# The scan loop of a gated SSM with mixture of experts: a step of one state and two channel chunks in place of two states and one chunk

## The chip, the cores and the metric

The kernel runs on one core of a Trainium2 chip. The metric is the device time of one execution, in microseconds (us). Line numbers (L482) are those of the kernel before; PE is TensorE, DVE is VectorE, ACT is ScalarE, POOL is GpSimd, SP is the engine that issues most DMAs. A number such as 128x1024 is partitions by elements, all float32.

## What is computed

A batch is 512 positions of 512 channels, and there are four batches. Cut to what matters (ssm and ffn are the two layers):

```
x = x + tanh(g_xattn) * ssm(ctx, z=layernorm(x))
x = x + tanh(g_ffn)   * ffn(layernorm(x))

ssm:  u = silu(conv4(in_proj @ ctx))              # 512 channels x 512 positions
      dt, B, C = x_proj @ u;  delta = softplus(dt_proj @ dt + bias)
      for each of 16 states n, along the positions t:
          state_n = state_n * exp(delta_t * A_n) + (delta_t * u_t) * B_t[n]
          y_t    += state_n * C_t[n]
      y = (y + D * u) * silu(z)
ffn:  shared(x) + sum over the 3 best of 7 experts of weight_e * expert_e(x)
      expert(x) = (silu(x @ w1) * (x @ wg)) @ w2   # all 512 x 512
```

## The kernel before

**Layout.** Channels lie on partitions, in four chunks of 128 (NC = 4), and positions along the free dimension. The state recurrence is one scan instruction of DVE along 512 positions for each state and chunk: 16 x 4 = 64 scans a batch.

**The scan loop** (`loop(b, sums)`, L434 on) makes 32 steps a batch. A step is a pair of states (g0, g0 + 1) of one chunk c; the four chunks follow each other within a pair of states. In a step:

- `product` (L509, POOL, 128x1024): B of both states times delta*u of the chunk, into one of two buffers `h`. It is issued one step ahead, so it waits until the buffer's last reader, an add of the step before, is done.
- `decay` (L514, L520, ACT, two of 128x512): exp(delta*A) for each state, into one of two PSUM banks `da`; an exp waits until the scan that read its bank is done.
- two scans (L540, DVE, 128x512), state by state.
- `finish`, issued with the next step: the multiply by C (L467, DVE, 128x1024), and the sum over states. In loop 0 (batch 0) PE sums, with two identity matmuls (L480) into a PSUM bank for each chunk. In loops 1 to 3 DVE sums, with two adds (L482, 128x512) into the same 512 columns of y.

B and C are broadcast to all partitions by a load of 1 MB for a pair of states (`load_bc`, L256 on), two pairs ahead. `ready` (L493) prepares a chunk when its first step comes: `rest_of_z` (L299, L300) and `soft` (L308, L309) on DVE finish delta, `d_u` (L314, ACT) puts D*u into y, `mul` (L321, DVE) makes delta*u. `gate` (L456, DVE) multiplies y by silu(z) at the end of a chunk. Small closures such as silus wait in a list `later` until `flush` issues them. In loops 1 to 3 the pieces of the next layer's preparation (`ahead`: in_proj, conv, x_proj, soft and so on) are issued between the steps.

**The experts** (`moe`, `post`, `route`, `experts`). For each batch q after its loop: `post` turns y by PE (L606), adds it to x and takes statistics on DVE (L610 to L612), normalizes (L615), turns the result back (L623) and copies it by ACT (L626). `route` computes gate logits (pl L670, lg L672, pg L676), the three best on DVE (L689 to L727), counts by PE (pc L718, L719) and scatters rows to expert tiles by indirect DMAs of POOL (L782). `experts` does the shared expert (p1s and p2s L827, the silu sgs L925, hidden L928, pos L960), then 13 tiles of routed rows: turn (L816), copy (L821), p1 and p2 (p, L827), silu (h, L1054), gating (h, L999), turn and copy of h, po (L827), scaling (yo, L860, ACT) and an adding indirect DMA (L865, POOL). After the last full tile stands an If (L878) for the rest. Below, po_12 or h_12 is that of tile 12.

**The order** is written out by hand: each engine gets its instructions in the order in which the program issues them, and executes them in that order. `front` prepares batch 0, loop 0 runs alone, and then a small planner at the end of the kernel merges two generators, the slots of `moe` and the steps of `ssm`: each slot has a PE cost and a DVE cost, each step returns its DVE cost (3.6 in loop 0, 4.95 in the others, and what is issued with it), and steps are issued while their sum lags behind PE's (`while tV < tP`). So loops 1, 2 and 3 interleave with the experts of batches 0, 1 and 2, and the experts of batch 3 run alone.

```
    for slot in moe():
        ...
        tP += slot[0]
        tV += slot[1]
        must = len(slot) > 2 and slot[2]
        while tV < tP or must:
            must = False
            d = next(steps, None)
```

Of the kernel before, what the change touches and what calls it, by code (L numbers as in the profile page):

```python
# [16 lines left out]
P = 128  # L17
# [6 lines left out]
NG = 2  # L24
I32 = mybir.dt.int32
# [7 lines left out]
def gated_ssm_moe(  # L33
# [170 lines left out]
    class Layer:  # L204
# [51 lines left out]
        def load_bc(self, g0):  # L256
            bc = two.tile([P, 2, NG, L], F32, tag="bc", name=f"bc_{self.b}_{g0}")
            nc.sync.dma_start(bc, self.rows[:, g0 : g0 + NG, :].partition_broadcast(P))
            self.bcs[g0] = bc
# [107 lines left out]
    def front():  # L367


        l0, l1 = layers[0], layers[1]  # L370
        for c in range(NC):
            l0.in_proj(c)
        for c in range(2):
            l1.in_proj(c)
        for c in range(NC):
            l0.conv(c)
            if c > 0:
                l0.silu(c - 1)
        l0.silu(NC - 1)
        for c in range(2):  # L380
            l1.conv(c)
        l0.x_proj()
        l0.rows_out()
        l0.load_bc(0)
        l0.load_bc(NG)
        for c in range(NC):
            l0.dt_proj(c)
        l1.in_proj(2, ps_a.tile([P, L], F32, tag="da", name="pin_1_2"))
        l1.in_proj(3, ps_s.tile([P, L], F32, tag="s", name="pin_1_3"))
        for c in range(NC):  # L390
            l0.abs_relu(c, by_vector=True)
        for c in range(NC):
            l0.exp(c)
        for c in range(NC):
            l0.log(c, own=False)
        norm_x(0)
        for c in range(NC):
            l0.rest_of_z(c)
        l0.soft(0)
        l0.mul(0)  # L400
        l1.conv(2)
# [32 lines left out]
    def loop(b, sums):  # L434
# [16 lines left out]
        steps = [(g0, c) for g0 in range(0, NS, NG) for c in range(NC)]  # L451
# [6 lines left out]
        def finish(n, h):  # L458

            g0, c = steps[n]  # L460
            bc = ly.bcs[g0]
            cost = 0.0
            if sums is not None and n >= NC:
                next(todo, 0.0)
                next(early, None)
            hc = h if sums is None else held[-1][:, n % 2]
            nc.vector.tensor_tensor(hc, h, bc[:, 1], ALU.mult)  # L467
            if sums is None:
                if b - 1 in shared_done:

                    left = max(n_todo - done[0], 0)
                    for _ in range(max(1, -(-left // max(1, len(steps) - NC - n)))):
                        done[0] += 1
                        cost += next(todo, 0.0)
                if nxt is not None and g0 + NG == NS and 0 < c <= nxt.n_du:
                    nxt.mul(c - 1)
                    cost += 0.7
            for j in range(NG):
                if sums is not None:
                    nc.tensor.matmul(sums[c], ident, hc[:, j, :], start=False, stop=(g0 + j == NS - 1))  # L480
                else:
                    nc.vector.tensor_tensor(y[:, c, :], y[:, c, :], h[:, j, :], ALU.add)  # L482
            if sums is not None and g0 + NG == NS and c > 0:
                gate(c - 1)
            if c == NC - 1:
                ly.bcs.pop(g0)
                if g0 + 2 * NG < NS:
                    ly.load_bc(g0 + 2 * NG)
                elif nxt is not None:
                    nxt.load_bc(g0 + 2 * NG - NS)  # L490
            return cost

        def ready(layer, n):  # L493

            g0, c = steps[n]
            cost = 0.0
            if g0 == 0 and layer.n_soft == c:
                layer.soft(c)
                cost += 1.4
            if g0 == 0 and layer.n_mul == c:  # L500
                layer.mul(c)
                cost += 0.7
            return cost

        def product(layer, n):

            g0, c = steps[n]
            h = two.tile([P, NG, L], F32, tag="h", name=f"h_{layer.b}_{g0}_{c}")
            nc.gpsimd.tensor_tensor(  # L509
                h, layer.bcs[g0][:, 0], layer.u[:, c, :].unsqueeze(1).to_broadcast([P, NG, L]), ALU.mult  # L510
# [3 lines left out]
        def decay(layer, n):  # L514

            g0, c = steps[n]
            layer.das[n] = []
            for k in range(g0, g0 + NG):
# [6 lines left out]
        for n, (g0, c) in enumerate(steps):  # L525
            cost = 3.6 if sums is not None else 4.95
# [9 lines left out]
            if sums is not None and g0 == 0:  # L536
                nc.tensor.matmul(sums[c], ident, y[:, c, :], start=True, stop=False)
            h = ly.hs.pop(n)
            for j, da in enumerate(ly.das.pop(n)):
                nc.vector.tensor_tensor_scan(h[:, j, :], da, h[:, j, :], 0.0, ALU.mult, ALU.add)  # L540
# [4 lines left out]
            elif nxt is not None and nxt.n_mul > 0:  # L545
                product(nxt, 0)
                decay(nxt, 0)
            if b == 0 and g0 == 0:
                if c == 0:
                    nxt.conv(NC - 1)  # L550
                    for k in range(NC):
                        later.append(lambda k=k: nxt.silu(k))
                    szs = silus_x(b)
                if c == 1:
                    flush()
            if g0 + NG == NS:
                if nxt is not None and nxt.n_soft == NC:
                    nxt.d_u(c)
                if c > 0 and sums is None:
                    flush()  # L560
                    gate(c - 1)
                    cost += 0.7
# [3 lines left out]
            if b > 0 and g0 == 10:  # L566
                norm_x(b, c)
                cost += 0.9
            if b > 0 and g0 == 12 and c == 1:
# [6 lines left out]
        gate(NC - 1)  # L576
# [551 lines left out]
    held[-1] = wpool.tile([P, 2, NG, L], F32, tag="w0", name="hc")  # L1128
# [70 lines left out]
```

## Time and profile before

| what | value |
|---|---|
| median of 3 runs | 1161.34 us (1160.76 to 1167.23) |
| profiled execution, its own time | 1164.13 us |
| its span (first to last instruction) | 1161.9 us |
| mean granted TensorE clock | 0.938 of full |
| PE, DVE busy from 180 to 951 us (771 us) | 660 and 643 us |
| a step of loop 0, scan to scan | 3.58 us |
| a step of loops 1 to 3 with nothing between | 4.96 us |

The span is the time that the trace covers; 2.2 us lie around it. Loop 0 ends near 179 us; the last step of loop 3 lies before 951 us, where the routing of batch 3 begins. In a profile line of the timeline the columns are: start, busy time (us), engine, line, operation, output<-inputs, size, count, and in brackets the idle time of the engine before it and what ended it.

### The profile page before, as it was taken

The numbers are of one execution on the slowest core, as the hardware profiler recorded it, in microseconds if no ns is written. First come the engines' busy times: TensorE is split into PE (matmuls) and PEld (weight loads), VectorE is DVE, ScalarE is ACT, GpSimd is POOL, SyncE is SP. The second block draws the span as 40 slices with busy tenths as digits, with TensorE's granted clock in tenths as the row PEclk, the third lists the DMA queues.
The fourth block names the chain that finished last, engine by engine and source line by source line (L and its number), as shares of the span: only waits on it lengthen the run. The fifth ranks groups of instructions, "written<-read, shape, count | busy, mean of one in ns | idle before, by whom it ended". The sixth has DMA issues, their size and how long they took to land. (4 is left out here: it accounts for less than half of the span.)

```text
span 1161.9 us, 8955 instructions
## 1 busy us (share of the span) xinstructions
PE 960.8 (83%) x2504; PEld 427.8 (37%) x2504; DVE 816.7 (70%) x1093; ACT 537.9 (46%) x747; POOL 470.7 (41%) x311
## 2 busy tenths in 40 slices
PE   7376555678799897986999994987998979999993
PEld 3122112333344443433444441433443534444441
DVE  5889996977889998866989996969999502100000
ACT  4565343253676774434586762435657220122211
POOL 0255651272344655451444644554666214011111
PEclk9689898889899998988999997988999999999998
DMA  4159221098499988387799975498999757899974
GB/s 126 46 178 377 113 72 55 14 348 290 152 315 303 300 292 234 118 314 238 246 311 322 353 225 144 173 301 273 316 349 345 219 175 247 299 346 325 332 226 101
DMA packets 138427, 276.30 MB, mean 238 GB/s; under 512 B 17262, under 2 KB 17262, under 8 KB 138110
## 3 DMA queue, kind: packets, MB, share of 16 engines
q1 hardware_dynamic: 126846, 248.91, 61.4%
q0 software_dynamic: 11328, 26.42, 9.9%
q8 instruction: 26, 0.43, 0.1%
q10 hardware_dynamic: 192, 0.26, 0.1%
q14 instruction: 35, 0.29, 0.1%
HBM read 234.85 MB, written 44.91 MB: 241 GB/s over the span
## 5 line engine op out<-in xcount | busy, mean ns | idle before, releaser
L509 POOL TENSOR_TENSOR h<-bc,home 128x1024 f32<-128x1024 f32 x128 | 304.5, 2380 | 376.2 <-DVE home L482 268.7
L827 PE MATMUL p<-w,turned_x 128*128 128x512 f32 x832 | 381.7, 603 | 22.6 <-ACT h L1054 18.7
L540 DVE TENSOR_TENSOR_SCAN h<-da,h 128x512 f32<-128x512 f32 x256 | 298.3, 1207 | 18.6 <-POOL h L509 13.1
L520 ACT ACTIVATE da<-home,a_neg 128x512 f32<-128x512 f32 x256 | 174.5, 689 | 281.8 <-DVE h L540 279.4
L827 PEld LDWEIGHTS p<-w,turned_x 128*128 128x128 f32 x832 | 155.0, 193 | 206.1 <-issue 172.7
L827 PE MATMUL po<-w,turned_h 128*128 128x512 f32 x416 | 190.1, 600 | 19.3 <-ACT yo L860 16.4
L865 POOL DMA_INDIRECT acc<-yo,row x52 | 93.3, 1794 | 220.4 <-ACT yo L860 168.8
L482 DVE TENSOR_TENSOR home<-home,h 128x512 f32<-128x512 f32 x192 | 132.6, 691 | 5.9
L999 DVE TENSOR_TENSOR h<-h,p 128x512 f32<-128x512 f32 x52 | 35.1, 675 | 143.5 <-PE p L827 142.3
L467 DVE TENSOR_TENSOR h<-h,bc 128x1024 f32<-128x1024 f32 x96 | 130.6, 1360 | 1.1
L480 PE MATMUL sum<-hc,ident 128*128 128x512 f32 x128 | 69.5, 669 | 56.4 <-DVE hc L467 56.4
L827 PEld LDWEIGHTS po<-w,turned_h 128*128 128x128 f32 x416 | 75.7, 192 | 98.4 <-issue 75.9
L821 ACT COPY turned_x<-pt_x 128x512 f32<-128x512 f32 x52 | 30.2, 581 | 103.8 <-PE pt_x L816 103.7
L960 PE MATMUL pos<-w_s,home 128*128 128x512 f32 x128 | 66.2, 674 | 10.5 <-DVE home L928 7.8
L782 POOL DMA_INDIRECT xs<-xn,place x48 | 56.7, 1182 | 29.1 <-issue 15.9
L827 PE MATMUL p1s<-home,w_s 128*128 128x512 f32 x128 | 61.6, 626 | 5.5 <-ACT sgs L925 5.5
L520 ACT ACT_TABLE_LOAD x51 | 65.4, 1283 | 0.9
L860 ACT ACTIVATE yo<-po,weight 128x512 f32<-128x512 f32 x52 | 35.6, 684 | 62.2 <-PE po L827 48.6
L480 PEld LDWEIGHTS sum<-hc,ident 128*128 128x128 f32 x128 | 23.6, 205 | 101.5 <-DVE hc L467 79.4
L827 PE MATMUL p2s<-home,w_s 128*128 128x512 f32 x128 | 57.5, 592 | 0.0
L233 DVE SCALAR_TENSOR_TENSOR home<-pin,pr,home 128x511 f32<-128x511 f32 (+2 forms) x48 | 35.7, 748 | 23.8 <-ACT home L229 22.7
L821 ACT COPY turned_h<-pt_h 128x512 f32<-128x512 f32 x52 | 30.0, 578 | 46.9 <-PE pt_h L816 46.9
(137 smaller groups left out, 810.1 us busy)
## 6 DMA issues: line engine op xcount, KB each, us to landing
w<-in_w_dram SPq DMA_DIRECT2D x104, 1024.0 KB, 7.8
w<-in_wg_dram SPq DMA_DIRECT2D x52, 1024.0 KB, 8.7
bc<-rows SPq DMA_DIRECT2D x32, 1024.0 KB, 10.4
xt<-xs SPq DMA_DIRECT2D x52, 256.0 KB, 5.6
xs<-empty SPq DMA_DIRECT2D x6, 1560.0 KB
w_s<-in_ws_dram SPq DMA_DIRECT2D x8, 1024.0 KB, 9.4
xx<-in_x_dram SPq DMA_DIRECT2D x4, 1024.0 KB, 11.1
w_s<-in_wsg_dram SPq DMA_DIRECT2D x4, 1024.0 KB
```

What stands on the lines that cost most here:

```text
L233: nc.vector.scalar_tensor_tensor(xc[:, k:], pin[:, 0 : L - k], pr[:, c, last - k : last - k + 1], xc[:, k:], ALU.mult, ALU.add,)
L467: nc.vector.tensor_tensor(hc, h, bc[:, 1], ALU.mult)
L480: nc.tensor.matmul(sums[c], ident, hc[:, j, :], start=False, stop=(g0 + j == NS - 1))
L482: nc.vector.tensor_tensor(y[:, c, :], y[:, c, :], h[:, j, :], ALU.add)
L509: nc.gpsimd.tensor_tensor(h, layer.bcs[g0][:, 0], layer.u[:, c, :].unsqueeze(1).to_broadcast([P, NG, L]), ALU.mult)
L520: nc.scalar.activation(da, layer.delta[:, c, :], AF.Exp, scale=a_neg[:, c, k : k + 1])
L540: nc.vector.tensor_tensor_scan(h[:, j, :], da, h[:, j, :], 0.0, ALU.mult, ALU.add)
L782: put = nc.gpsimd.indirect_dma_start(xs[q % 2], bass.IndirectOffsetOnAxis(ap=place[:, t, k : k + 1], axis=0), xns[:, t, :], None)
L821: nc.scalar.copy(t, pt)
L827: nc.tensor.matmul(p[:, 0:n], lhs(c), rhs(c), start=(c == 0), stop=(c == NC - 1))
L865: nc.gpsimd.indirect_dma_start(acc, bass.IndirectOffsetOnAxis(ap=slot_of[q][1][:, i : i + 1], axis=0), yo, None, compute_op=ALU.add,)
L960: nc.tensor.matmul(pos[t], hTs[:, c, ts(t, P)], ws.t[2][:, c, :], start=(c == 0), stop=(c == NC - 1))
```

## The change

A step becomes one state k of two neighbouring chunks c0 and c0 + 1 (W = 2). There are 32 steps as before. For each load of B and C the order is (first state, chunks 0 and 1), (second state, chunks 0 and 1), (first, 2 and 3), (second, 2 and 3). The product and the multiply by C read one state's row for both chunks. The two scans of a step write two chunks, so in loops 1 to 3 one add of 128x1024 into two chunks of y takes the place of two adds of 128x512; in loop 0 the two matmuls of a step go to two banks. With this:

- `front` does soft and mul of chunks 0 and 1 before conv(2) (before: chunk 0 alone), and `ready` does two chunks at a time, also at the end of loop 0.
- the gates come later: in loop 0 those of chunks 0 and 1 with the last step but one, in loops 1 to 3 those of 0 and 1 with the last two steps, and those of 2 and 3 at the end.
- D*u and delta*u of the next layer are made in the last three steps, one a step and two in the last.
- the planner's cost of a step of loops 1 to 3 is 4.8 in place of 4.95.

The diff in full:

```diff
--- before.py
+++ after.py
@@ -22,6 +22,7 @@
 TOPK = 3
 EPS = 1e-5
 NG = 2
+W = 2
 I32 = mybir.dt.int32
 
 CW, CB, DTB, DD, AL = 0, 4, 5, 6, 7
@@ -256,7 +257,7 @@
         def load_bc(self, g0):
             bc = two.tile([P, 2, NG, L], F32, tag="bc", name=f"bc_{self.b}_{g0}")
             nc.sync.dma_start(bc, self.rows[:, g0 : g0 + NG, :].partition_broadcast(P))
-            self.bcs[g0] = bc
+            self.bcs[g0 // NG] = bc
 
 
 
@@ -396,8 +397,9 @@
         norm_x(0)
         for c in range(NC):
             l0.rest_of_z(c)
-        l0.soft(0)
-        l0.mul(0)
+        for c in range(W):
+            l0.soft(c)
+            l0.mul(c)
         l1.conv(2)
 
 
@@ -448,7 +450,11 @@
             todo = ahead(nxt)
         n_todo, done = 1 + NC + (NC + 2) + 2 * (NC // 2), [0]
         szs = None
-        steps = [(g0, c) for g0 in range(0, NS, NG) for c in range(NC)]
+
+        steps = [
+            (g0 + j, c0) for g0 in range(0, NS, NG) for c0 in range(0, NC, W) for j in range(NG)
+        ]
+        per_load = NG * NC // W
 
         def gate(c):
 
@@ -457,73 +463,79 @@
 
         def finish(n, h):
 
-            g0, c = steps[n]
-            bc = ly.bcs[g0]
+            k, c0 = steps[n]
+            i = n % per_load
             cost = 0.0
-            if sums is not None and n >= NC:
+            if sums is not None and n >= per_load:
                 next(todo, 0.0)
                 next(early, None)
             hc = h if sums is None else held[-1][:, n % 2]
-            nc.vector.tensor_tensor(hc, h, bc[:, 1], ALU.mult)
+            c_k = ly.bcs[k // NG][:, 1, k % NG, :]
+            nc.vector.tensor_tensor(hc, h, c_k.unsqueeze(1).to_broadcast([P, W, L]), ALU.mult)
             if sums is None:
                 if b - 1 in shared_done:
 
                     left = max(n_todo - done[0], 0)
-                    for _ in range(max(1, -(-left // max(1, len(steps) - NC - n)))):
+                    for _ in range(max(1, -(-left // max(1, len(steps) - per_load - n)))):
                         done[0] += 1
                         cost += next(todo, 0.0)
-                if nxt is not None and g0 + NG == NS and 0 < c <= nxt.n_du:
-                    nxt.mul(c - 1)
+                if nxt is not None and n >= last - W and nxt.n_mul < nxt.n_du:
+                    nxt.mul(nxt.n_mul)
                     cost += 0.7
-            for j in range(NG):
-                if sums is not None:
-                    nc.tensor.matmul(sums[c], ident, hc[:, j, :], start=False, stop=(g0 + j == NS - 1))
-                else:
-                    nc.vector.tensor_tensor(y[:, c, :], y[:, c, :], h[:, j, :], ALU.add)
-            if sums is not None and g0 + NG == NS and c > 0:
-                gate(c - 1)
-            if c == NC - 1:
-                ly.bcs.pop(g0)
-                if g0 + 2 * NG < NS:
-                    ly.load_bc(g0 + 2 * NG)
+            if sums is None:
+                nc.vector.tensor_tensor(y[:, c0 : c0 + W, :], y[:, c0 : c0 + W, :], h, ALU.add)
+            else:
+                for w in range(W):
+                    nc.tensor.matmul(sums[c0 + w], ident, hc[:, w, :], start=False, stop=(k == NS - 1))
+                if n == last - 1:
+                    for c in range(NC - W):
+                        gate(c)
+            if i == per_load - 1:
+                ly.bcs.pop(k // NG)
+                g = k // NG + 2
+                if g * NG < NS:
+                    ly.load_bc(g * NG)
                 elif nxt is not None:
-                    nxt.load_bc(g0 + 2 * NG - NS)
+                    nxt.load_bc(g * NG - NS)
             return cost
 
         def ready(layer, n):
 
-            g0, c = steps[n]
+            k, c0 = steps[n]
             cost = 0.0
-            if g0 == 0 and layer.n_soft == c:
-                layer.soft(c)
-                cost += 1.4
-            if g0 == 0 and layer.n_mul == c:
-                layer.mul(c)
-                cost += 0.7
+            for c in range(c0, c0 + W):
+                if k == 0 and layer.n_soft == c:
+                    layer.soft(c)
+                    cost += 1.4
+                if k == 0 and layer.n_mul == c:
+                    layer.mul(c)
+                    cost += 0.7
             return cost
 
         def product(layer, n):
 
-            g0, c = steps[n]
-            h = two.tile([P, NG, L], F32, tag="h", name=f"h_{layer.b}_{g0}_{c}")
+            k, c0 = steps[n]
+            h = two.tile([P, W, L], F32, tag="h", name=f"h_{layer.b}_{k}_{c0}")
+            b_k = layer.bcs[k // NG][:, 0, k % NG, :]
             nc.gpsimd.tensor_tensor(
-                h, layer.bcs[g0][:, 0], layer.u[:, c, :].unsqueeze(1).to_broadcast([P, NG, L]), ALU.mult
+                h, b_k.unsqueeze(1).to_broadcast([P, W, L]), layer.u[:, c0 : c0 + W, :], ALU.mult
             )
             layer.hs[n] = h
 
         def decay(layer, n):
 
-            g0, c = steps[n]
+            k, c0 = steps[n]
             layer.das[n] = []
-            for k in range(g0, g0 + NG):
+            for c in range(c0, c0 + W):
                 da = ps_a.tile([P, L], F32, tag="da", name=f"da_{layer.b}_{k}_{c}")
                 nc.scalar.activation(da, layer.delta[:, c, :], AF.Exp, scale=a_neg[:, c, k : k + 1])
                 layer.das[n].append(da)
 
         last = len(steps) - 1
         h_before = None
-        for n, (g0, c) in enumerate(steps):
-            cost = 3.6 if sums is not None else 4.95
+        for n, (k, c0) in enumerate(steps):
+            i = n % per_load
+            cost = 3.6 if sums is not None else 4.8
             if h_before is not None:
                 cost += finish(n - 1, h_before)
             if n not in ly.hs:
@@ -533,47 +545,50 @@
                 decay(ly, n)
             if n < last:
                 cost += ready(ly, n + 1)
-            if sums is not None and g0 == 0:
-                nc.tensor.matmul(sums[c], ident, y[:, c, :], start=True, stop=False)
+            if sums is not None and k == 0:
+                for c in range(c0, c0 + W):
+                    nc.tensor.matmul(sums[c], ident, y[:, c, :], start=True, stop=False)
             h = ly.hs.pop(n)
-            for j, da in enumerate(ly.das.pop(n)):
-                nc.vector.tensor_tensor_scan(h[:, j, :], da, h[:, j, :], 0.0, ALU.mult, ALU.add)
+            for w, da in enumerate(ly.das.pop(n)):
+                nc.vector.tensor_tensor_scan(h[:, w, :], da, h[:, w, :], 0.0, ALU.mult, ALU.add)
 
             if n < last:
                 product(ly, n + 1)
                 decay(ly, n + 1)
-            elif nxt is not None and nxt.n_mul > 0:
+            elif nxt is not None and nxt.n_mul >= W:
                 product(nxt, 0)
                 decay(nxt, 0)
-            if b == 0 and g0 == 0:
-                if c == 0:
-                    nxt.conv(NC - 1)
-                    for k in range(NC):
-                        later.append(lambda k=k: nxt.silu(k))
-                    szs = silus_x(b)
-                if c == 1:
-                    flush()
-            if g0 + NG == NS:
-                if nxt is not None and nxt.n_soft == NC:
+            if b == 0 and n == 0:
+                nxt.conv(NC - 1)
+                for c in range(NC):
+                    later.append(lambda c=c: nxt.silu(c))
+                szs = silus_x(b)
+            if b == 0 and n == 1:
+                flush()
+            if nxt is not None and nxt.n_soft == NC and n >= last - W and nxt.n_du < NC:
+
+                ready_du = (c0 + W) if n < last else NC
+                for c in range(nxt.n_du, min(nxt.n_du + (1 if n < last else W), ready_du)):
                     nxt.d_u(c)
-                if c > 0 and sums is None:
-                    flush()
-                    gate(c - 1)
-                    cost += 0.7
+            if n >= last - 1 and sums is None:
+                flush()
+                gate(n - last + 1)
+                cost += 0.7
             h_before = h
             if n == 2 and b > 0 and nxt is not None:
                 ctxs[b + 1] = load_ctx(b + 1)
-            if b > 0 and g0 == 10:
-                norm_x(b, c)
+            if b > 0 and k // NG == 5:
+                norm_x(b, i)
                 cost += 0.9
-            if b > 0 and g0 == 12 and c == 1:
+            if b > 0 and k // NG == 6 and i == 1:
                 szs = silus_x(b)
             yield cost
         if b == 0:
             for c in range(NC):
                 nxt.log(c, own=False)
         cost = finish(last, h_before)
-        gate(NC - 1)
+        for c in range(NC - W, NC):
+            gate(c)
         if b == 0:
             cost += ready(nxt, 0)
             product(nxt, 0)
@@ -1125,7 +1140,7 @@
 
 
 
-    held[-1] = wpool.tile([P, 2, NG, L], F32, tag="w0", name="hc")
+    held[-1] = wpool.tile([P, 2, W, L], F32, tag="w0", name="hc")
     front()
     held[0] = shared_weights(0)
     early = first_loads()
```

## The prediction

> **What bounds the kernel now.** I read busy times, then windows by stage, then the timeline inside one step and at each long wait of PE.
>
> ```profile
> PE 960.8 (83%) x2504; PEld 427.8 (37%) x2504; DVE 816.7 (70%) x1093; ACT 537.9 (46%) x747; POOL 470.7 (41%) x311
> L482 DVE TENSOR_TENSOR home<-home,h 128x512 f32<-128x512 f32 x192 | 132.6, 691 | 5.9
> ```
> ```profile
> 300.00:400.00 100.00, 95.29 (x258) 42.50 (x257) 91.89 (x111) 68.89 (x97) 48.21 (x24) 0.98 0.86 285
> 500.00:600.00 100.00, 86.71 (x208) 37.22 (x209) 76.42 (x90) 52.13 (x72) 38.68 (x23) 0.90 0.78 266
> 700.00:800.00 100.00, 75.14 (x184) 32.15 (x184) 76.50 (x120) 37.76 (x50) 48.84 (x40) 0.90 0.67 212
> 960.00:1060.00 100.00, 99.33 (x271) 46.51 (x270) 15.00 (x46) 14.59 (x26) 17.93 (x28) 1.00 0.89 304
> ```
>
> Window columns: length, busy PE, PEld, DVE, ACT, POOL, clock, DMA share, GB/s. Four stages follow. Until about 180 us loop 0 runs alone and DVE sets the pace. From 180 to 951 loops 1 to 3 are interleaved with the experts of batches 0 to 2. In mid-batch (300:400) PE is at 95 and DVE at 92 of 100: balanced, PE slightly ahead. At the changes of batch (700:800) both are near 76: there the two wait for each other by turns. From 951 the last batch is PE alone (99 of 100); no scan step is left there, so those 211 us can't change. The two adds that the change merges (132.6 us) are thus on DVE, which binds alone only in loop 0, where those adds don't exist (PE sums there). What can move is PE's idle time between 180 and 951. Its long waits:
>
> ```profile
> 236.50 1.22 PE L827 MATMUL p1s<-home,w_s 128*128 128x512 f32 x1 [4.75 <-ACT sgs L925]
> 456.19 0.47 PE L623 MATMUL pn<-ident,xn 128*128 128x128 f32 x1 [5.98 <-ACTq L878]
> 710.02 1.22 PE L827 MATMUL po<-w,turned_h 128*128 128x512 f32 x1 [11.40 <-ACT yo L860]
> 802.60 1.22 PE L827 MATMUL p<-w,turned_x 128*128 128x512 f32 x1 [8.47 <-ACT h L1054]
> ```
>
> and, of about 8 to 10 us each, pn at 190.92, pc at 215.51, and pin at 297.21 and 537.89. After such a wait PE is also slow: the eight matmuls from 802.60 take 5.53 us, the usual eight 3.60 (782.38), so a long wait costs some 1.9 us more than itself.
>
> **The change, part by part.**
>
> *The wide add.* One step of loops 1 to 3:
>
> ```profile
> 782.95 1.23 DVE L467 TENSOR_TENSOR h<-h,bc 128x1024 f32<-128x1024 f32 x1
> 784.22 1.42 DVE L482 TENSOR_TENSOR home<-home,h 128x512 f32<-128x512 f32 x2
> ```
>
> Two adds of 512 are busy 1.42 us and the next scan starts 1.33 us after them; the C multiply, the nearest row to an add of 128x1024, is busy 1.23 and has its follower after 1.27. So a step saves between 1.33-1.27=0.06 and 1.42-1.23=0.19; I take 0.12. Times 96 steps: 6 to 18 us, 12 taken, all DVE work. The multiply and the product now read one state's row twice instead of two rows; the route's L708 (broadcast operand) and L709 (none) both take 0.36, so that costs 0. Scans, exps, loads of B and C, and loop 0's matmuls keep number and size. POOL's product of the next step starts when the adds end (780.67, product 780.75) and ends under the scans (783.1): it moves with them, 0.
>
> How much of the 12 is on the path: in mid-batch PE leads, so only a part of it arrives. Tiles of batch 0: about 23 steps lie there, 23 x 0.12 = 2.8, of which I take 2; batch 1: 1; batch 2 below.
>
> *Start of loop 0.* soft and mul of chunk 1 go ahead of conv(2): about 2.2 us more DVE before POOL's first product, but followed instruction by instruction the first scan starts at 44.55 instead of 44.29, since other things were late too. The wait of 5.03 us for chunk 3's D*u at 63.68 goes; step 3's exp now stands behind the same flush of silus on ACT, so its scan starts at some 67.45 instead of 67.86. Net -0.4 (+-1). The rest of the loop keeps 3.58 us a step, and its last gate waits for PE either way (178.55).
>
> *Handover 0 to 1.* The last gate is followed by `ready`, now for two chunks. The extra block L299 to L321 takes 3.40 us (179.16 to 182.56) and stands ahead of add_y, xn, pn, pl and pg: all +3.4. Against it, this goes:
>
> ```profile
> 200.25 0.69 DVE L321 TENSOR_TENSOR home<-home,home 128x512 f32<-128x512 f32 x1 [5.50 <-ACT home L314]
> ```
>
> (chunk 1's D*u stood behind the copies of xn and lg on ACT; the scan of step 1, and on DVE the route, stood behind that). Chunk 2's D*u will stand behind lg in its place, some 2 us. By the sum +3.4-5.5+2 = -0.1 the route starts as before (211.15 against 211.47 when I follow each instruction); but chunk 3's block of 3.3 us no longer stands between route and hidden(0), so the sigmoids come about 4.1 earlier (231.7 against 235.85) and the 4.75 us wait at 236.50 shrinks to about 1. So -4.1 at best.
>
> Here a rule speaks against the change. POOL's product for step 1, held by chunk 1's mul until now (201.09), is free to start right after the iota (190.39+3.4=193.8), in the same moment as xn (L615, tensor_scalar). The Trainium skill, page "SBUF — State Buffer", section "Who interferes with whom", says that DVE and GpSimd share a port pair under an exclusive lock, and that tensor_scalar may take it: the second to start is blocked for the first one's whole length. Rows:
>
> ```profile
> 746.13 2.36 POOL L509 TENSOR_TENSOR h<-bc,home 128x1024 f32<-128x1024 f32 x1
> 746.23 3.35 DVE L467 TENSOR_TENSOR h<-h,bc 128x1024 f32<-128x1024 f32 x1
> ```
>
> A multiply begun just after the product took 3.35 instead of 1.23, as the lock would have it; but at 455.29 xn began 0.54 us after the product of 452.59 to 454.93 had ended, so no row shows xn beside one. By the lock xn loses up to 2.35 (pn, and the route behind it, too) and the handover gives -1.8; if xn gets in first, -4.1. I take -2.5, range -4 to 0.
>
> *Batch 0 to 1.* Put in order, the last gating (h_12) now stands behind two scan steps and two add_y on DVE, and on ACT turned_h_12 and yo_11 stand behind the exps of step (1, chunks 2 and 3), which wait for scans that end about 454. po_12 then starts at 456 instead of 446.50 and PE stands about 8 us; pn's wait of 5.98 is partly absorbed by it. pl moves from 460.78 to about 465 or 466: +4.5 (range 0 to +8). It is what the trace shows one batch later:
>
> ```profile
> 707.07 0.69 ACT L520 ACTIVATE da<-home,a_neg 128x512 f32<-128x512 f32 x1 [7.00 <-DVE h L540]
> 709.29 0.69 ACT L860 ACTIVATE yo<-po,weight 128x512 f32<-128x512 f32 x1
> ```
>
> An exp waits 7.00 us for a scan to free its PSUM bank, and the yo behind it, which PE needs at 710.02, waits with it.
>
> *Batch 1 to 2.* There turn_y and pn now come before the last outputs: the 11.40 us wait splits into two shorter ones and the matmuls after it stay quick. Followed from h_11: pg at +38.8 instead of +42.8; -5 with the following matmuls (range -6 to +2).
>
> *Tiles of batch 2.* Steps stand 3 to 4 earlier relative to tiles (planner's 4.8), the last step some 18 us earlier. The wait of 8.47 stays, split 3.4 and 5; p_4's 1.25 and the later .67, .63 and 3.09 (889.39) go: 5.6 at most, -3 taken.
>
> *Sum:* -0.4-2.5-2+4.5-1-5-3 = -9.4. The profiled execution took 1164.13 (span 1161.9 and 2.2 around it); the sum is its difference. The median of the runs shown is 1161.34, so 1161.34-9.4 = 1152.0.
>
> **Rivals.**
>
> *Stronger.* The stall at batch 0 to 1 fails to appear (0 instead of +4.5) and the handover gives its whole -4.1: -9.4-4.5-1.6 = -15.5; with the full 18 us of adds, of which half arrives (9 instead of the 3 counted), -21.5: 1140 to 1146, middle 1143. For it: 700:800 has a quarter of both engines idle. Against: PE's 95 in 300:400.
>
> *Only moved.* Waits change places and PE, already leading, gives nothing back; DMA helps that (at 800:870 it is .95 busy with 320 GB/s, so tiles can't hurry): 1161. Against: the 5.50 and 4.75 us waits are lost work in the order itself.
>
> *Slower.* ACT's queue at the boundaries. If, at 0 to 1, turned_h and yo stand behind exps as at 710.02 in full, this costs 11.4+1.9 = 13.3 and not 4.5; and if the 1 to 2 boundary keeps its 11.4 (0 instead of -5): -9.4+8.8+5 = +4.4; and if that later order also makes a second silu or h wait like 802.60 (8.47+1.9=10.4): +14.8, 1176. It decides once the exps wait for scans over 7 us at both boundaries. For it: exps wait 279.4 us for scans in all, 7.2 at the longest. Against: most of these waits hold up nobody, since PE is idle only 111 us between 180 and 951 (771 less 660 busy), of which the three behind ACT shown make 25.
>
> **From cases to numbers.** As summed .42 (1152, own range 1146 to 1159); stronger .24 (1143); only moved .15 (1161); slower .19 (1176). One per cent, about what a measurement here can tell from no change, is 11.6 us: faster below 1149.7, slower above 1173. Faster: .17 of the .42 and all but .01 of the .24 = .40; slower: .16 of the .19, = .16; same .44. Range 1138 (stronger with most of its adds) to 1174, which leaves out about .2.
>
> **What would show it.** The adds as x96 of 128x1024 at 1.2 to 1.3 us; if about 1.4, no DVE is saved. p1s's wait at the handover under 2 us; xn near 1.9 for four, or 4 if blocked. A PE wait of 6 to 9 us before po_12 near 450; none of over 8 near 700. The last stage, from pl of batch 3 to the end, 211 us in both. I am wrong if that stage changes, if loop 0's step isn't 3.58, or if a wait at a boundary is longer than 11 us.

## The result and the profile after

The changed kernel takes 1171.4 us (median of 10 runs, 1168.71 to 1173.89) where the kernel before takes 1162.49 in the runs beside it: a ratio of 1.0071, 95% interval 1.0055 to 1.0086. It is slower by 0.7%, where 1152.0 was forecast. Line numbers from here on are those of the changed kernel: L474 is the multiply by C, L486 the add, L489 loop 0's sums, L520 the product, L531 the exps, L553 the scans, L630 xn, L685 pl, L704 and L731 the route's s and sel, L733 pc, L842 the experts' matmuls, L875 yo, L880 the adds of rows, L893 the If, L940 the silu sgs of the shared expert, L1069 the tiles' silu. In the experiments an edit shifts the lines behind it by one to three; e2, e10 and e14 have those of the kernel before.

The profile of the changed kernel, its busy times and the groups that answer to those of before:

```profile
PE 978.5 (83%) x2504; PEld 432.3 (37%) x2504; DVE 808.7 (69%) x997; ACT 534.3 (46%) x744; POOL 467.8 (40%) x311
L553 DVE TENSOR_TENSOR_SCAN h<-da,h 128x512 f32<-128x512 f32 x256 | 298.2, 1206 | 39.2 <-POOL h L520 29.1
L486 DVE TENSOR_TENSOR home<-home,h 128x1024 f32<-128x1024 f32 x96 | 117.4, 1223 | 2.7
```

The wide add does what it says: 117.4 us busy instead of 132.6. DVE has less to do and waits more: before its scans stand 39.2 us of idle time, mostly for POOL's product (29.1; before, 18.6 and 13.1). And PE executes the same 2504 matmuls in 978.5 us instead of 960.8. The windows shown before, after the change:

```profile
300.00:400.00 100.00, 96.30 (x262) 43.04 (x261) 88.49 (x96) 69.29 (x97) 50.83 (x23) 0.98 0.89 299
500.00:600.00 100.00, 87.19 (x211) 36.89 (x209) 80.69 (x83) 54.11 (x73) 44.38 (x29) 0.91 0.80 273
700.00:800.00 100.00, 77.00 (x184) 32.94 (x182) 78.02 (x108) 41.41 (x55) 53.21 (x42) 0.88 0.62 203
960.00:1060.00 100.00, 98.42 (x261) 44.60 (x260) 17.48 (x57) 16.28 (x26) 18.97 (x28) 0.98 0.82 279
```

In mid-batch (first line) DVE is down from 91.89 to 88.49 and PE leads as before. Windows of equal length don't say where the 10.2 us of longer span (1172.1 against 1161.9) lie. For that I cut both spans at the same PE instructions: the end of loop 0, the first pos of a batch that waits for hidden, one matmul p among the later tiles of batch 0 (381.82 and 379.79 are the same one), and pl of each batch. One execution of each stands for its kernel here; the changed kernel's (1173.89 us) is the slowest of its ten, so 10.2 is a little more than the 8.9 between the medians. Columns: length, busy PE, clock, DMA share, GB/s. Before:

```profile
178.30:248.63 70.33, 43.62 (x117) 0.85 0.30 107
248.63:381.82 133.19, 116.61 (x300) 0.95 0.81 276
381.82:460.78 78.96, 70.84 (x208) 0.94 0.88 274
460.78:501.38 40.60, 36.40 (x85) 0.95 0.51 174
501.38:720.78 219.40, 189.55 (x509) 0.93 0.81 271
720.78:760.97 40.19, 36.01 (x84) 0.96 0.55 190
760.97:950.99 190.02, 168.45 (x477) 0.96 0.87 286
950.99:1161.90 210.91, 191.96 (x528) 0.97 0.81 262
```

After:

```profile
178.40:246.93 68.53, 43.39 (x117) 0.82 0.31 107
246.93:379.79 132.86, 119.23 (x300) 0.94 0.83 282
379.79:466.90 87.11, 73.78 (x209) 0.92 0.76 247
466.90:506.43 39.53, 35.88 (x85) 0.95 0.55 192
506.43:725.23 218.80, 191.57 (x508) 0.93 0.78 258
725.23:772.42 47.19, 36.76 (x85) 0.92 0.58 196
772.42:959.06 186.64, 171.58 (x476) 0.95 0.90 291
959.06:1172.10 213.04, 193.90 (x528) 0.97 0.80 261
```

Line by line the lengths differ by -1.8, -0.3, **+8.2**, -1.1, -0.6, **+7.0**, -3.4 and +2.1. The loss lies in two stages, with 15.2 us between them: the third (last tiles of batch 0 to pl of batch 1) and the sixth (pl to pos of batch 2). The others together give 5 us back; the 2.1 of the last one are no matter of the change, since the same stage takes 210.2 us in run e4 below and 212.7 in e3. In those two PE's idle time (length less busy) grows by 5.2 and 6.3 us; elsewhere it shrinks or stays (0.2 more in the last), so that in sum PE is idle 2.5 us less. What is left is the busy column: +12.6 us for the same matmuls, at a lower clock in five of the eight lines and a higher one in none. The mean granted clock is 0.925 instead of 0.938.

*Stage three.* po_12 in the kernel before, then two lines of ACT and po_12 in the changed kernel, near the end of batch 0:

```profile
446.50 3.70 PE L827 MATMUL po<-w,turned_h 128*128 128x512 f32 x8 [0.18 <-ACT yo L860]
```

```profile
453.54 0.69 ACT L531 ACTIVATE da<-home,a_neg 128x512 f32<-128x512 f32 x1 [8.87 <-DVE h L553]
455.75 0.69 ACT L875 ACTIVATE yo<-po,weight 128x512 f32<-128x512 f32 x1
456.49 5.40 PE L842 MATMUL po<-w,turned_h 128*128 128x512 f32 x8 [3.90 <-ACT yo L875]
```

An exp waits 8.87 us for a scan, yo stands behind it, and po_12 behind yo: it starts at 456.49 instead of 446.50, and its eight matmuls take 5.40 us instead of 3.70. Before, po_12 was past when PE came to wait for pn (at 456.19); now pn follows po_12, at 462.76, and pl follows pn.

*Stage six.* POOL, then DVE, then PE, at the change from batch 1 to 2:

```profile
726.41 1.55 POOL L880 DMA_INDIRECT acc<-yo,row  x1 [8.34 <-ACTq L893]
733.10 1.53 POOL L880 DMA_INDIRECT acc<-yo,row  x1 [5.13 <-DMA acc<-yo,row]
734.49 4.82 POOL L520 TENSOR_TENSOR h<-bc,home 128x1024 f32<-128x1024 f32 x2
737.04 2.34 DVE L553 TENSOR_TENSOR_SCAN h<-da,h 128x512 f32<-128x512 f32 x2 [15.68 <-POOL h L520]
739.30 0.16 DVE L704 TENSOR_REDUCE s<-pg 128x4 f32<-128x28 f32 x1
743.33 0.60 PE L733 MATMUL pc<-sel,before 128*128 128x28 f32 x2 [6.26 <-DVE sel L731]
```

The last add of rows waits for the DMA of the one before it; the product of the next scan step stands behind both on POOL, the scan behind the product (15.68 us idle), the routing behind the scan on DVE (s at 739.30, although PE was done with pg by 730.0), and PE waits for sel. The same places in the kernel before:

```profile
722.01 2.46 POOL L509 TENSOR_TENSOR h<-bc,home 128x1024 f32<-128x1024 f32 x1
727.29 0.19 DVE L689 TENSOR_REDUCE s<-pg 128x4 f32<-128x28 f32 x1 [12.14 <-PE pg L676]
734.15 0.30 PE L718 MATMUL pc<-sel,before 128*128 128x28 f32 x2
```

There the last add of rows started 12.5 us earlier (720.56), and the routing stood ahead of the scan on DVE: s follows pg at once, and PE does not wait for sel.

### The profile page after: what moved, and what is told of

Read it like the earlier page. It is cut to its first block, busy times and chain, and to the rows that moved or that the text cites. A ratio compares the mean times of both kernels' runs of the same rounds, so it can differ in the third digit from the quotient of the medians.

```text
span 1172.1 us, 8859 instructions
## 1 busy us (share of the span) xinstructions
PE 978.5 (83%) x2504; PEld 432.3 (37%) x2504; DVE 808.7 (69%) x997; ACT 534.3 (46%) x744; POOL 467.8 (40%) x311
## 5 line engine op out<-in xcount | busy, mean ns | idle before, releaser
L520 POOL TENSOR_TENSOR h<-bc,home 128x1024 f32<-128x1024 f32 x128 | 306.9, 2401 | 349.7 <-DVE home L486 242.7
L842 PE MATMUL p<-w,turned_x 128*128 128x512 f32 x832 | 386.5, 609 | 20.0 <-ACT h L1069 17.1
L553 DVE TENSOR_TENSOR_SCAN h<-da,h 128x512 f32<-128x512 f32 x256 | 298.2, 1206 | 39.2 <-POOL h L520 29.1
L531 ACT ACTIVATE da<-home,a_neg 128x512 f32<-128x512 f32 x256 | 174.2, 689 | 298.5 <-DVE h L553 296.6
L842 PEld LDWEIGHTS p<-w,turned_x 128*128 128x128 f32 x832 | 157.7, 196 | 206.1 <-issue 179.2
L842 PE MATMUL po<-w,turned_h 128*128 128x512 f32 x416 | 195.2, 614 | 19.2 <-ACT yo L875 16.3
L880 POOL DMA_INDIRECT acc<-yo,row x52 | 92.9, 1786 | 253.2 <-ACT yo L875 190.7
L474 DVE TENSOR_TENSOR h<-h,bc 128x1024 f32<-128x1024 f32 x96 | 130.8, 1363 | 1.2
L486 DVE TENSOR_TENSOR home<-home,h 128x1024 f32<-128x1024 f32 x96 | 117.4, 1223 | 2.7
L489 PE MATMUL sum<-hc,ident 128*128 128x512 f32 x128 | 71.8, 688 | 51.9 <-DVE hc L474 51.7
L842 PEld LDWEIGHTS po<-w,turned_h 128*128 128x128 f32 x416 | 77.5, 197 | 101.5 <-issue 78.7
L875 ACT ACTIVATE yo<-po,weight 128x512 f32<-128x512 f32 x52 | 35.5, 683 | 73.6 <-PE po L842 57.5
L842 PE MATMUL p1s<-home,w_s 128*128 128x512 f32 x128 | 62.5, 633 | 1.0 <-ACT sgs L940 1.0
L489 PEld LDWEIGHTS sum<-hc,ident 128*128 128x128 f32 x128 | 24.0, 208 | 98.7 <-DVE hc L474 77.1
L842 PE MATMUL p2s<-home,w_s 128*128 128x512 f32 x128 | 57.5, 592 | 0.0
```

What stands on the lines that cost most here:

```text
L474: nc.vector.tensor_tensor(hc, h, c_k.unsqueeze(1).to_broadcast([P, W, L]), ALU.mult)
L486: nc.vector.tensor_tensor(y[:, c0 : c0 + W, :], y[:, c0 : c0 + W, :], h, ALU.add)
L489: nc.tensor.matmul(sums[c0 + w], ident, hc[:, w, :], start=False, stop=(k == NS - 1))
L520: nc.gpsimd.tensor_tensor(h, b_k.unsqueeze(1).to_broadcast([P, W, L]), layer.u[:, c0 : c0 + W, :], ALU.mult)
L531: nc.scalar.activation(da, layer.delta[:, c, :], AF.Exp, scale=a_neg[:, c, k : k + 1])
L553: nc.vector.tensor_tensor_scan(h[:, w, :], da, h[:, w, :], 0.0, ALU.mult, ALU.add)
```

## Experiments

Each is the changed kernel with the edit shown, unless it says otherwise. All compute the same result. Ratios are to the kernel before on the same chip, with 95% intervals; the changed kernel's own is 1.0071 [1.0055, 1.0086].

### The planner's cost and the step's shape, apart

**e1**: `cost = 3.6 if sums is not None else 4.95` (4.8 before the edit).

> The changed kernel with the planner's cost of a step put back from 4.8 to 4.95; nothing else. Theory (the loss lies in the order at the two changes of batch: at batch 0 to 1 two exps stand ahead of turned_h_12 and yo_11 on ACT, at batch 1 to 2 four exps stand ahead of yo_9): with 4.95 the program's order has yo_11 ahead of the exps at 0 to 1 and yo_9 ahead of them at 1 to 2, so both boundaries lose less: 1160 to 1166 us, with the wide add kept. Rival 1 (the wide add or the row read twice costs time in each step): no gain, 1169 to 1174. Rival 2 (the steps come too slowly or too fast for the tiles, whatever stands at the boundaries): a change of less than 3 us.

1159.54 us, ratio 0.9991 [0.9974, 1.0009]. A little under the theory's range: the wide step with the old cost is as fast as the kernel before. Both long stages shrink: from pos of batch 0 to pl of batch 1 it takes 215.81 us (220.0 in the changed kernel), and from pl of batch 2 to pos 39.24 (47.19). At the second the product is back at 722.21, the routing runs ahead of the scan, and PE has no wait for sel:

```profile
249.51:465.32 215.81, 189.10 (x509) 0.94 0.82 274
722.70:761.94 39.24, 35.59 (x85) 0.96 0.55 190
735.79 0.30 PE L733 MATMUL pc<-sel,before 128*128 128x28 f32 x2
```

**e2**: the kernel before with 4.8 in place of 4.95.

> The kernel before with the planner's cost at 4.8 in place of 4.95; step shape and adds as before. Theory (order at the boundaries, set by the planner): yo_11 at batch 0 to 1 comes to stand behind two exps, and h_12 and yo_10 at 1 to 2 behind six and eight, as in the changed kernel, so it is slower than before by some 4 to 10 us: 1167 to 1173. Rival 1 (the step's new shape costs the time): within 2 us of before, 1161 to 1165.

1183.64 us, ratio 1.0192 [1.0175, 1.0209]: slower by more than expected. At the boundary of batch 1 to 2 po waits 13.35 us for turned_h:

```profile
718.65 5.96 PE L827 MATMUL po<-w,turned_h 128*128 128x512 f32 x8 [13.35 <-ACT turned_h L821]
```

At equal cost the new shape is thus not the slower one: at 4.8 it has 1.0071 against 1.0192, at 4.95 0.9991 against 1.

**e7, e8, e12**: 5.0, 5.2 and 5.4 in place of 4.8.

> The changed kernel with a planner's cost of 5.0. The program's order on ACT at both boundaries is then nearly that of the kernel before (at 1 to 2: yo_9, h_12, two exps, yo_10, turned_h_11, four exps, turned_h_12, yo_11). Theory (the order at the boundaries decides, and the step's new shape itself gains): like the kernel before or up to 8 us faster, 1154 to 1162. Rival (a larger cost makes the steps come too late and loop 3 ends into batch 3): 1165 or more.

1160.81 us, ratio 0.9978 [0.9965, 0.9991].

> The changed kernel with a planner's cost of 5.2. The program's order on ACT at 1 to 2 has yo_10, turned_h_11, turned_h_12 and yo_11 ahead of the exps; at 0 to 1 two exps stand ahead of yo_10. Theory: po's long wait at 1 to 2 goes (8 to 11 us), the wait at 0 to 1 stays about 5: 1150 to 1158. Rival (steps too late: loop 3 runs into the end of batch 2, whose post can then not overlap the tiles): 1165 to 1175.

1140.73 us, ratio 0.9807 [0.9784, 0.9830]: a larger gain than the theory gave.

> The changed kernel with a planner's cost of 5.4. At 1 to 2 all of ACT's work for the tiles stands ahead of loop 3's exps from yo_10 on, but two more exps stand ahead of yo_9 and h_12. Theory (the position decides, not the size of the cost): between 5.0 and 5.2 in its waits, 1140 to 1152. Rival (a larger cost is simply better): below 1138. Rival (steps too late): above 1155.

1166.41 us, ratio 1.0032 [1.0007, 1.0056]: above the theory's range, and in that of its last rival. By cost 4.8, 4.95, 5.0, 5.2, 5.4 the new shape gives 1.0071, 0.9991, 0.9978, 0.9807, 1.0032. The time does not follow the cost in one direction. That it depends on where the steps fall among the last tiles is how I read this, but ACT's order alone did not forecast it: 1140 to 1152 was expected at 5.4.

**e10**: the kernel before with 5.2.

> The kernel before, with a planner's cost of 5.2 in place of 4.95. Theory (what counts is which steps stand ahead of the last tiles' work on ACT; the step's shape gains a few us on top): clearly faster than before, with 3 to 12 us left to the changed shape at the same cost: 1143 to 1153. Rival 1 (the shape gains nothing): 1138 to 1143. Rival 2 (the gain at 5.2 belongs to the new shape alone): 1158 to 1166.

1174.16 us, ratio 1.0112 [1.0073, 1.0151]: outside the theory's range, beyond the second rival's. A cost that is good for one shape is not good for the other; here pn waits for xn, 9.34 us at batch 1 (464.79) and longer at batch 2:

```profile
727.46 3.55 PE L623 MATMUL pn<-ident,xn 128*128 128x128 f32 x16 [13.02 <-DVE xn L615]
```

The kernel before was run at three costs only, so whether another one would help it as 5.2 helps the new shape is not known.

### The wide add alone

**e3**, and **e16** on top of e11 below:

```diff
-                nc.vector.tensor_tensor(y[:, c0 : c0 + W, :], y[:, c0 : c0 + W, :], h, ALU.add)
+                for w in range(W):
+                    nc.vector.tensor_tensor(y[:, c0 + w, :], y[:, c0 + w, :], h[:, w, :], ALU.add)
```

> The changed kernel with two adds of 128x512 in place of the one of 128x1024; the planner and the order are those of the changed kernel. It does the same sums. Theory: the adds are busy 132 us instead of 117, all on DVE, and 2 to 6 us of the 15 reach the end, at the boundaries where scans are waited for: 1173 to 1178. Rival 1 (a wide add holds back POOL or ACT and is the cause of the loss): faster than the changed kernel, 1160 to 1168.

1175.1 us, ratio 1.0104 [1.0083, 1.0124]: by the medians 3.7 us more than with the wide add; the intervals overlap by a little, so this is not clear of noise.

> The kernel of e11 (cost 5.2, ACT's work first) with two adds of 128x512 in place of the wide one, same order. Theory: 15 us more of DVE work, of which DVE's share of the waits (a quarter to a half) arrives: 1139 to 1144. Rival (the wide add carries nothing): 1135 to 1138.

1141.06 us, ratio 0.9812 [0.9788, 0.9836], against 0.9788 [0.9748, 0.9828] with the wide add: the intervals overlap, so by itself it is unclear, though it points the same way. In neither run is the kernel faster without the wide add, so the add isn't the cause of the loss.

### The waits at the boundaries, one by one

**e4**: yo of the ninth tile ahead of four exps on ACT at batch 1 to 2.

```diff
+            if i == last_tile:
+                out(i - 3)
             yield SLOT, 0.7
-            if i > 2:
+            if 2 < i < last_tile:
                 out(i - 3)
```

> The changed kernel with one thing moved: the scaling yo of tile 9 of each batch is issued with the first slot of the last tile instead of the second, so that on ACT at batch 1 to 2 it stands ahead of four exps that wait for scans; at the other batches ACT's order stays. Theory: po_10 starts at about 700 instead of 708, the load of the last tile's w2 and the shared weights behind it start about 8 us earlier and are past when the adds of rows 10 to 12 are written, the product behind those adds on POOL comes earlier, and the route of batch 2 by 4 to 9 us: 1162 to 1168. Rival 3 (POOL's product is late for another reason than those adds, such as the load of B and C): 1169 to 1172.

1166.13 us, ratio 1.0040 [1.0026, 1.0053]: better than the changed kernel by 0.3%. Its trace at the place of stage six:

```profile
698.88 3.60 PE L842 MATMUL po<-w,turned_h 128*128 128x512 f32 x8
727.84 4.83 POOL L520 TENSOR_TENSOR h<-bc,home 128x1024 f32<-128x1024 f32 x2
730.40 2.34 DVE L553 TENSOR_TENSOR_SCAN h<-da,h 128x512 f32<-128x512 f32 x2 [10.53 <-POOL h L520]
736.69 0.38 PE L733 MATMUL pc<-sel,before 128*128 128x28 f32 x2 [1.21 <-DVE sel L731]
```

po_10 runs at 698.88 instead of 708.09 and in 3.60 us instead of 6.58; the product behind the adds comes 6.7 us earlier, and PE waits 1.21 instead of 6.26 for sel. Stage six takes 42.15 us (765.80 less 723.65) instead of 47.19.

**e13**: e4 with more of ACT's work put ahead of the exps (at the end of the last tile's third slot); **e14**: this part alone in the kernel before, at its own 4.95.

```diff
             if i == last_tile:
+                out(i - 2)
+                copy_h(i - 1)
                 W[i].load(2)
...
         gated(i)
-        out(i - 2)
-        copy_h(i - 1)
         output(i - 1)
```

> The changed kernel at its own cost of 4.8, with yo of tile 9 in the last tile's first slot and yo of tile 10 and the turned h of tile 11 at the end of its third slot, so that they stand ahead of the exps on ACT. Theory (ACT's queue at the boundaries is most of the loss): po's waits of 3.99 at 455 and 4.87 at 712 (both still there with yo_9 alone early) shrink, 1158 to 1164 us. Rival (the rest is POOL's adds ahead of the product and DVE's chain of scans): no better than with yo_9 alone, 1164 to 1168.

1170.62 us, ratio 1.0050 [1.0036, 1.0065]: above both ranges, and by the ratios not told apart from e4. pg is 3.5 us earlier than in the changed kernel (726.11), but the scan still waits for its product, and PE more for sel:

```profile
734.30 2.34 DVE L553 TENSOR_TENSOR_SCAN h<-da,h 128x512 f32<-128x512 f32 x2 [12.83 <-POOL h L520]
740.60 0.60 PE L733 MATMUL pc<-sel,before 128*128 128x28 f32 x2 [7.01 <-DVE sel L731]
```

> The kernel before (two states of one chunk, cost 4.95), with yo of tile 10 and the turned h of tile 11 issued at the end of the last tile's third slot. At batch 1 to 2 this takes two exps from ahead of them. Theory (the stall of 11.40 us at 710 is ACT's queue and no matter of the step's shape): 1152 to 1158 us. Rival (po_10 waits there for yo_9's bank and the scans; the time moves to pn): 1159 to 1164.

1164.9 us, ratio 1.0014 [0.9997, 1.0031]: no change, and the wait of 11.40 us for yo is still there at 709.32. I had taken the wrong instruction: the po that waits there is po_12, and it needs turned_h_12 and yo_11 (708.81 and 709.29 on ACT in the kernel before), which this move leaves behind the exps. The run thus says nothing of that wait; it says that the moved part alone is worth nothing in the kernel before.

**e5** was to put the routing of batch 2 ahead of the scan, but the step moved only into the routing's middle (PE still waits 2.99 us for sel), so it does not test this.

```diff
-        yield part, 0.0
+        yield (0.0 if q == 2 else part), 0.0
...
-            yield part, (2.8 if hc == 1 else 0.0), True
+            yield (2 if q == 2 and hc == 2 else 1) * part, (2.8 if hc == 1 else 0.0), (q != 2 or hc > 0)
```

> The changed kernel with one scan step of loop 3 moved behind the routing of batch 2 on DVE (the first slots of that batch ask for no step; the cost is given back two slots later). In the changed kernel that scan waits 15.68 us for a product that stands on POOL behind the adds of rows of tiles 10 to 12, and the routing stands behind the scan. Theory: the routing runs at about 730 as soon as pg is there, PE's wait of 6.26 us for sel goes, and up to 8 us are gained: 1163 to 1167 us. Rival (the wait only moves to the next thing that the late scan holds, such as hidden or the first tile): 1169 to 1173.

1174.72 us, ratio 1.0097 [1.0070, 1.0123]: nothing gained.

**e9** holds the steps back until the whole routing is through (the same two lines for hc 0 and 1, their cost given back behind them); **e15** is e9 and e13 together.

> The changed kernel with the whole routing of batch 2, from s to the positions, ahead of the scan steps on DVE (the slots of that stretch ask for no step and their cost is given back behind it). It mends the run before, in which the step had moved only into the middle of the routing. Theory (the adds on POOL make a product late, the scan behind it makes the routing late): sel comes about 4 us after pg and PE's wait of 6.26 us for it goes: 1163 to 1167 us. Rival (PE is then late for pg itself, or the held steps make hidden late): 1168 to 1173.

1174.05 us, ratio 1.0095 [1.0061, 1.0129]. The rival holds, with 1 us more. The wait for sel is gone, and others have come up further on:

```profile
739.30 0.30 PE L733 MATMUL pc<-sel,before 128*128 128x28 f32 x2
757.88 2.92 PE L842 MATMUL p1s<-home,w_s 128*128 128x512 f32 x3 [4.24 <-ACT sgs L940]
805.91 6.28 PE L842 MATMUL p<-w,turned_x 128*128 128x512 f32 x8 [6.36 <-ACT h L1070]
```

The silu that PE waits for at 757.88 is executed at 757.23, behind the exps of the held steps at 754.11 and 755.23.

> The changed kernel at cost 4.8 with ACT's moves of e13 and the routing of batch 2 ahead of the scan steps as in e9. Theory (two queues, ACT and then POOL with DVE, set the boundary one after the other): the wait of 7.01 us for sel goes and at least half of it arrives: 1160 to 1166 us. Rival (the held scan steps are needed soon after and give it back, as in e9): 1168 to 1174.

1168.57 us, ratio 1.0061 [1.0043, 1.0078]: not told apart from the changed kernel. The rival holds here too: the wait for sel is gone (pc at 730.24), and behind it PE waits 4.25 and 3.05 us for the shared expert's silus (748.83 and 760.51).

### The best version

**e6**: cost 4.95 with the edit of e14; **e11**: cost 5.2 with it.

> The changed kernel at cost 4.95, and with yo of tile 10 and the copy of the turned h of tile 11 issued at the end of the last tile's third slot, ahead of the exps of one or two scan steps on ACT (two at batch 0 to 1, four at 1 to 2). Theory: po_11's wait of 8.89 us for turned_h at 706 shrinks to 2 or less, PE's cold matmuls after it go too, and 5 to 9 us are gained on the kernel with cost 4.95: 1150 to 1156. Rival (ACT executes in order, so the copy that waits for PE's turn holds up the exps and the scans behind them by as much): 1158 to 1163.

1155.78 us, ratio 0.9950 [0.9931, 0.9970].

> The changed kernel at cost 5.2, and yo of tile 10 and the copy of the turned h of tile 11 issued ahead of the exps, as in the run at 4.95. It takes two exps from ahead of them at batch 0 to 1; at 1 to 2 nothing changes. Theory: po's wait of 4.45 us at 434.79 goes and 2 to 5 us are gained: 1135 to 1139. Rival (the boundary is set by xn, which waits for DVE: the time moves into pn's wait): 1139 to 1143.

1136.14 us, ratio 0.9788 [0.9748, 0.9828]: the fastest by its median, ahead of both kernels of the diff; its interval overlaps e8's. Four stages of e11, cut as above (pl to pos and pos to the next pl, for batches 1 and 2):

```profile
457.61:497.26 39.65, 36.00 (x85) 0.95 0.42 152
497.26:705.22 207.96, 186.77 (x508) 0.95 0.86 287
705.22:743.07 37.85, 34.19 (x85) 1.00 0.50 164
743.07:922.19 179.12, 168.97 (x476) 0.96 0.91 310
```

Here the tiles of batch 1 with the boundary after them take 208.0 us (218.8 in the changed kernel), the routing of batch 2 37.9 (47.2), and PE is busy 4.8 and 2.6 us less with them.

## Why the prediction failed, term by term

- **The wide add**: 0.12 us a step taken, 0.158 measured ((132.6 - 117.4) / 96). That the path sees only a part fits e3 (3.7 us of 15 by the medians, not clear of noise).
- **Start and loop 0**: -0.4 forecast, 0.0 measured (the turns of y start at 178.35 and 178.36).
- **Handover 0 to 1**: -2.5 forecast; pos comes 1.7 earlier (246.93 against 248.63) and tile 0 by 2.5. Right, and with the rule of the Trainium skill that I weighed ("SBUF — State Buffer", "Who interferes with whom": the one of VectorE and GpSimd that issues first holds the shared ports for its whole instruction, and the other is blocked). Of the four xn beside a product one took 2.65 us, the other three 0.54 as before. Before, then after:

```profile
190.32 1.92 DVE L615 TENSOR_SCALAR xn<-xx,mv_f,rstd_f 128x512 f32<-128x512 f32 x4 [1.13 <-POOL rstd_f L200]
```
```profile
193.57 4.02 DVE L630 TENSOR_SCALAR xn<-xx,mv_f,rstd_f 128x512 f32<-128x512 f32 x4 [1.13 <-POOL rstd_f L201]
193.60 2.34 POOL L520 TENSOR_TENSOR h<-bc,home 128x1024 f32<-128x1024 f32 x1
```

  The 2.1 us lost are near the 2.35 that I gave for one block by the lock. The product keeps its 2.34, so it is xn that is held; starts 0.03 us apart don't tell which of the two issued first.
- **Tiles of batch 0**: -2 forecast, -0.3 measured. PE is idle 3.0 us less there, but its matmuls take 2.6 us more.
- **Batch 0 to 1**: +4.5 forecast, +8.2 measured. I had followed the order to po_12 at 456, and it came at 456.49; pl was to come at 465 or 466, and came at 466.90. The mechanism and the instants were right (the 8 us of standing came as 3.62, 0.92 and 3.90), the term was not: they are instants on a chain of scans and exps that is no earlier for what PE gained before, and I still subtracted those 4.9 us (0.4 + 2.5 + 2) in the sum. The scan for which the exp at 453.54 waits starts at 452.29, the one in its place before at 452.42, although PE was 2.0 us ahead at the cut before this stage. At this boundary an earlier gain of PE is only a longer wait.
- **Tiles of batch 1 and batch 1 to 2**: -1 and -5 forecast; the three stages from pl of batch 1 to pos of batch 2 give -1.1 - 0.6 + 7.0 = +5.3. This is the step that failed: 11.3 of the 19.5 us between the forecast sum (-9.4) and the measured one (+10.1). "Followed from h_11: pg at +38.8 instead of +42.8" held as far as it went: pg comes 36.8 after the gating of h_11 (692.81), though h_11 itself stands 3.7 us later behind pos of batch 1, and from that pos to pg it is 2.3 us less than before. But it stopped at pg and put what follows at nothing. It left out POOL: the adds of the last rows, the product behind them, and the scan that the new order puts ahead of the routing. From pg to pc it takes 13.73 us instead of 7.31, and from pc to pos 29.09 instead of 26.82. And "the 11.40 us wait splits into two shorter ones and the matmuls after it stay quick" was wrong in its second half: po after a wait of 7.74 us takes 6.58 us.
- **Tiles of batch 2**: -3 forecast, -3.4 measured, with the waits as forecast: the 8.47 became 4.71, 0.88 and 3.32, and of the later four 0.36 is left. The last scan starts 9.2 us earlier (892.5 instead of 901.7), which is 20.7 earlier relative to pos of batch 2; I had taken 18. PE's matmuls take 3.1 us more, which the sum did not have, so the close number is in part luck.
- **Last batch**: 0 forecast, +2.1 measured, in its busy column (193.90 against 191.96), with no step of the loop in it. By e3 and e4 above such a difference comes without a change there.

Most of the signs that I had named came as named (adds at 1.22 us, p1s's wait 0.52, xn 4.02, loop 0's step 3.58, no wait over 8 us near 700), and the time still went the other way: none of them looks at the routing of batch 2 behind pg.

Of the rivals, the slower one (1176, at .19) named one of the causes, ACT's queue at the boundaries with slow matmuls behind the waits. Its terms did not come as it had them (neither the 13.3 nor the 11.4 us in full, nor a second wait of 8.47), and POOL's queue, where stage six is lost, is not in it. The larger omission was to treat the planner's 4.8 as a shift of 3 to 4 steps in batch 2 alone. By e1 it carries the whole loss: with 4.95 the same shape is level with before.

Shown: the loss is in the two boundary stages, it comes with the cost of 4.8 and not with the wide step (e1, e3), and of its parts the late yo_9 is worth 0.3% (e4). Not settled is how the rest divides. Taking one wait away (e9, e13) or two (e15) gave nothing measurable more; their traces show the wait at the next place. That the delayed scan steps are needed soon after in any case is my reading of this, not a measurement.

## What to carry to other kernels

Where two engines are balanced and their order is merged by a list of costs, cost the merging constant as a change of its own and run it alone before the rest. A term won ahead of a point where the engine waits for another one's chain isn't carried past it: sum instants along the chain that is last there, with every queue on it, and not gains by stage. Follow that chain to the next instruction that the engine in the lead waits for, not to a point before it. When a wait is to be split, count also the matmuls after each of the parts.

## What was not expected of the hardware

The kernel lost 10.2 us of span although PE was idle less: from loop 0 to the end its idle time fell by 2.5 us and its busy time rose by 12.6 us for the same matmuls. After some waits stand slow groups (eight matmuls in 5.40 us after 3.90 of waiting, 6.58 after 7.74, against 3.60 in an unbroken run); not after each: behind the 3.09 us at 889.39 in the kernel before they took 3.70. A kernel's PE idle time alone did not rank these two.
